# Keys and queries by a second level of seven products, and what was moved to make room for it

## The chip, the cores and the metric

The kernel runs on one core of a Trainium2 chip. The metric is the device time of one execution in microseconds (us); 2714.67 us is the median of three runs before (2713.76 to 2714.91). A core has TensorE (PE, with its weight loads shown as PEld), VectorE (DVE), ScalarE (ACT), GpSimd (POOL) and the queue of SyncE (SP), from which most DMAs are issued. The engines run side by side and wait for each other through semaphores.

## The reference

Two layers over 32 graphs (the batch b) of 512 nodes with 512 features, all in float32. The first is attention with 8 heads of 64, masked by the adjacency; the second is a graph convolution. Each is added to its input and normalized. `_layernorm(x)` takes the mean and variance of a row.

```python
def reference(x, adj, Wq, bq, Wk, bk, Wv, bv, weight, bias):
    # layer 0
    q, k, v = ((x @ W + c).reshape(b, n, 8, 64) for W, c in ((Wq, bq), (Wk, bk), (Wv, bv)))
    scores = einsum('bihd,bjhd->bhij', q, k) / sqrt(64) + where(adj == 0, -1e9, 0)
    out = einsum('bhij,bjhd->bihd', softmax(scores), v).reshape(b, n, 512)
    x = _layernorm(x + out)
    # layer 1
    norm_adj = adj * deg_inv_sqrt[:, None] * deg_inv_sqrt[None, :]
    x = _layernorm(x + einsum('nm,bmo->bno', norm_adj, x @ weight) + bias)
    return x
```

## The kernel before

Every product of two 512x512 matrices (x by Wk, Wq, Wv, and the convolution's z by W1) is done by the method of seven products: both factors are cut into four halves' blocks of 256x256, sums and differences of blocks are kept beside the blocks (slots 0 to 6 of `XT`, `wk`, `wqv`, `w1`), and seven block products take the place of eight. One of these is called a half product here. It is done by matmuls with 128 rows of weights and 256 moving columns, and its result is read out of a PSUM bank by a *put* (ACT) or an *add* (DVE) into each output block that it belongs to. The tables `CHAIN` (L325), `LEAF` (L352) and `OUTER` (L353) give the order of the products, the banks ("A", "D", "B") in which they are accumulated, and the puts and adds after each; `seven` (L360) turns a table into a list of steps.

For the values (`values_of`, L382) and for the convolution of the inner batches, four of the seven half products, those of the blocks (1,1), (3,2), (2,3) and (4,4), are each done once more by seven, on blocks of 128x128. One step does the same *quarter product* for all four, by four matmuls of 128 moving columns into one bank; seven such steps (`quarters_of`, L410, table `LEAF`) take the place of the four half products, whose factors are 128-wide quarters (`QUARTERS`, made by `quarter`, L170, and the weights' by `weigh_quarter`, L258). The other three half products follow by table `OUTER`. For keys and queries (`keys_and_queries`, L438) all seven half products are done, for r = 0 and r = 1, each with K (weights `wk`) and Q (weights `wqv`) in the two halves of one bank; ACT's put adds the bias.

Wk stays in SBUF. The buffer `wqv` holds Wq or Wv in turn; `swap(0)` and `swap(1)` (L266) load the one or the other with its sums from DRAM, on SP.

The main loop (L898) runs over b and keeps three batches in flight: attention of b, the normalization and convolution of b-1, and the second normalization and stores of b-2. One pass has four stages on TensorE:

1. the first stretch (`stretch`, L529): for two of four groups of two heads, `scores` (PE, DVE's masked copy `e`, ACT's exponential), then `values` (PE) and `unload_values` (DVE's transpose into the one buffer `yb`, and SP's DMAs from `yb` into `yT`). `accumulate` (L481) sums the numerators `e` on POOL into `acc`;
2. keys and queries of b+1. Beside them are played, at numbered steps: `rest` and `store` of b-2 (statistics, `roots`, L574, ACT's normalization, SP's stores), the addition of the residual to b-1 (`add`, POOL), the `fold` (L543, DVE) of the two sums, `measure` and `root` of b-1, `quarters` of x, `norm` (ACT, two passes), `judge` (three small instructions of DVE that check the range of `inv`) and `low` (DVE, `lo`), and the gather that adds b1;
3. the second stretch, for the other two groups;
4. the first convolution product, the values of b+1 and the second convolution product (`convolve`, L709), with the folds of the second stretch, the scaling of the attention's output by `inv` (ACT), the loads of x for b+2 and of the residual, and POOL's sums of blocks.

Within an engine the order is the order of the program text: the wrapper `InOrder` pins every instruction to it. So a waiting instruction holds all that stand behind it on its engine. Waits come from the tile framework, which follows the use of every buffer and PSUM bank. The banks are handed out in turn:

```python
    def bank(shape, name="mm"):
        psum["n"] += 1
        return psum["pool"].tile(shape, F32, name=name, tag=f"bank{-psum['n'] % 8}", bufs=1)

    def pair(name):
        return psum["pool"].tile([P, 2, N], F32, name=name, tag="pair", bufs=4)
```

`banks(kind)` closes the pool and opens the next over the same eight banks: four pairs for the scores, eight single ones for products.

Of the kernel before, what the change touches and what calls it, by code (L numbers as in the profile page):

```python
# [18 lines left out]
P = 128  # L19
# [31 lines left out]
def unshifted(  # L51
# [21 lines left out]
    LAST = B - 1  # L73
    tensor, vector, scalar, gpsimd, sync = (
# [41 lines left out]
    columns = consts.tile([P, 12, 2, DT], F32, name="columns")  # L116
    XT = consts.tile([P, 11, 2, HALF], F32, name="xT")
    QUARTERS = XT[:, 7:].rearrange("p k u o -> p k (u o)").rearrange("p k (n o) -> p k n o", o=P)
# [51 lines left out]
    def quarter(at):  # L170
        old, new = XT[:, 1:5].rearrange("p k u (t o) -> p k u t o", t=2), QUARTERS
        to, a, c = (
            (1, old[:, :, 0, 1], old[:, :, 0, 0]), (2, old[:, :, 1, 1], new[:, 1]),
            (3, old[:, :, 1, 1], old[:, :, 0, 1]), (0, old[:, :, 1, 0], new[:, 2]),
        )[at]
        gpsimd.tensor_tensor(new[:, to], a, c, ALU.subtract)

    def quarters():
        for at in range(4):
            quarter(at)  # L180

    R = {}

    def load_residual(b):
        if b < LAST:
            t = acts.tile([P, NT, D], F32, name="xr", tag="zT", bufs=1)
        else:
            t = wk[:, 3:].rearrange("p k u o -> p k (u o)")
        R[b] = [t[:, i, :] for i in range(NT)]
        for i in range(NT):  # L190
            sync.dma_start(R[b][i], x[b, ts(i, P), :])
        return [lambda: gather(t, rows(bv))]
# [11 lines left out]
    def load_parts(w, name, engine, t=None, pieces=PIECES):  # L204
        if t is None:
            t = consts.tile([P, 7, 2, HALF], F32, name=name)
        for i, q in pieces:
            engine.dma_start(
                t[32 * q : 32 * (q + 1), 2 * i : 2 * i + 2].rearrange("r j u o -> r (j u) o"),
                w[ts(q, P), ts(i, HALF)].rearrange("(t r) o -> r t o", r=32),  # L210
            )
        return t
# [11 lines left out]
    def load_row(v, name, engine):  # L224
        t = consts.tile([P, v.shape[0]], F32, name=name)
        engine.dma_start(t, bass.AP(tensor=v.tensor, offset=v.offset, ap=[[0, P], [1, v.shape[0]]]))
        return t
# [25 lines left out]
    b1_r = load_row(b1, "b1_r", nc.sync)  # L253
    wv_quarters = consts.tile([P, 3, 4, P], F32, name="wv_quarters")
    w1_quarters = consts.tile([P, 3, 4, P], F32, name="w1_quarters")
    stored = [drams.tile([P, 7, 2, HALF], F32, name=f"{name}_parts") for name in ("wq", "wv", "w1")]
# [9 lines left out]
    def swap(k):  # L266
        sync.dma_start(wqv, stored[k])
# [7 lines left out]
    minus_half = consts.tile([P, NT], F32, name="minus_half")  # L275
    gpsimd.memset(minus_half, -0.5)
    half = consts.tile([P, NT], F32, name="half")
    gpsimd.memset(half, 0.5)
    sel = consts.tile([P, 2, 32], F32, name="sel")
# [16 lines left out]
    consts.tile([P, 88], F32, name="margin")  # L296
# [85 lines left out]
    def values_of(b):  # L382
# [23 lines left out]
        left = lambda k, s: XT[:, s, k % 2, ts(k // 2, P)] if k in (0, 1, 3) else QUARTERS[:, max(k - 3, 0), s - 1]  # L406
        leaf, _ = quarters_of(left, w, wv_quarters, lambda: V[b], lambda: out(0, 0))
# [29 lines left out]

    def keys_and_queries(b, r):  # L438
        def multiply(p, i, j, fresh):
            for c, w in enumerate((wk, wqv)):  # L440
                for u in range(2):
                    tensor.matmul(
                        p[:, c, :], w[:, i, u, ts(r, P)], XT[:, j, u, :],
                        start=fresh and c == 0 and u == 0, stop=u == 1, skip_group_check=True,
                    )

        def out(i, j):
            if (b, ORDER[0]) not in KQ:
                for g in ORDER:
                    KQ[b, g] = acts.tile([P, 2, N], F32, name="kq", bufs=6)  # L450
            return KQ[b, r + 2 * i][:, :, ts(j, HALF)]

        def put(q, p):
            g = r + 2 * q[0]
            for c in range(2):
                scalar.activation(out(*q)[:, c], p[:, c], AF.Identity, bias=bias[:, c, g : g + 1], scale=1.0)

        def add(q, p):
            vector.tensor_add(out(*q), out(*q), p)

        return seven(CHAIN if b else PLAIN_FIRST, multiply, put, add)

# [17 lines left out]

    def accumulate(b, g):  # L481
        e = E[b, g]
        if b < LAST:
            a = work.tile([P, 2, N], F32, name="acc", bufs=2)
            gpsimd.tensor_add(a, e[0], e[1])
            for j in range(2, NT):
                gpsimd.tensor_add(a, a, e[j])
            ACC[b, g] = [a]
            return
        ACC[b, g] = []  # L490
        for l in range(2):
# [7 lines left out]
            ACC[b, g].append(a)  # L499

# [28 lines left out]
    def stretch(b, gs, gap=()):  # L529
# [3 lines left out]
        for g in gs:  # L533
            accumulate(b, g)
        banks("products")
        for g in gs:
            av = bank([P, N], "av")
            values(b, g, av)
            unload_values(b, g, av)
            if g == gs[0]:  # L540
                run(gap)

    def fold(b, g):  # L543
        a = ACC.pop((b, g))[0]
        if g == ORDER[0]:
            SM[b] = small.tile([P, H, N // 32], F32, name="folded")
# [26 lines left out]

    def roots(mv, eps):  # L574
# [14 lines left out]
    def finish(b):  # L589
        t = {}  # L590

        def inverse_all():
# [5 lines left out]
            t["inv"] = small.tile([P, NT, H], F32, name="inv")  # L598
# [7 lines left out]
        def inverse(c, p):  # L606
# [4 lines left out]
            if c == 0:  # L611
                t["inv"] = small.tile([P, NT, H], F32, name="inv")
# [3 lines left out]
        def judge():  # L616
            inv = t["inv"].rearrange("p i h -> p (i h)")
            low = small.tile([P, NT * H], F32, name="low")
# [38 lines left out]
        def root(i=0, k=NT):  # L657
            rstd, add = roots(t["mv"][:, i : i + k], None)
# [3 lines left out]
        def norm(i):  # L662
            if b not in HI:
                if b < LAST:
                    HI[b] = acts.tile([P, NT, D], F32R, name="hi", bufs=1)
                    lo = acts.tile([P, NT, D], F32R, name="lo", bufs=1)
                    LO[b] = [lo[:, k, :] for k in range(NT)]
                else:
                    HI[b] = acts.tile([P, NT, D], F32R, name="hi2", tag="v", bufs=1)
                    lo = [acts.tile([P, 2, D], F32R, name="lo2", tag="kq", bufs=6) for _ in range(2)]  # L670
                    LO[b] = [lo[k // 2][:, k % 2, :] for k in range(NT)]
# [37 lines left out]
    def convolve(b):  # L709
# [59 lines left out]
        def begin():  # L769
# [5 lines left out]
            if b == LAST - 2:  # L775
                t["whole"] = XT[:, 7:].rearrange("p k u o -> p k (u o)")
# [65 lines left out]
        def root(n, k):  # L842
            t[n] = roots(t["mv"][:, n : n + k], eps2[:, n : n + k])
# [43 lines left out]
    nc.sync.dma_start(stored[1], NUM[:, :4].rearrange("p e k (u o) -> p (e k) u o", u=2)[:, :7])  # L887
# [10 lines left out]
    for b in range(B):  # L898
# [7 lines left out]
        stretch(b, one, late + back["measure"][:3] if back else ())  # L906
# [12 lines left out]
        if b < LAST:  # L919
            k0, k1 = keys_and_queries(b + 1, 0), keys_and_queries(b + 1, 1)  # L920
            main = [p for pair in zip(k0, k1) for p in pair]
            if b == 0:
                ahead_x = acts.tile([P, 2, 2, N], F32, name="x2", tag="lo", bufs=1)
# [9 lines left out]
            else:  # L933
                measure, norm, low = ahead["measure"], ahead["norm"], ahead["low"]
                loads = [lambda b=b: biased.extend(load_residual(b))]
                scale = ahead["inverse"] + ahead["scale"] if b == 1 else []
                beside = {
                    0: rest + scale + ahead["add"], 1: store[:1] + fold0, 2: store[1:2], 3: store[2:3] + fold1,
                    4: store[3:] + measure[:2] + (loads if b == LAST - 1 else []), 5: measure[2:] + ahead["root"] + [quarters],
                    7: norm[:1] + ahead["judge"], 8: norm[1:2] + low[:1] + ([lambda: run(biased)] if b == LAST - 1 else []),  # L940
                    9: norm[2:3] + low[1:2], 10: norm[3:] + low[2:3],
                    11: low[3:] + ahead["lift_all"],
# [13 lines left out]
        if b < LAST:  # L956
            swap(1)
        stretch(b, two, f[b]["pairs"][0] + f[b]["pairs"][1] if b == LAST else ())
# [6 lines left out]
        if b < LAST:  # L965
            end = f[b]
            if b == 0:
                fourth = acts.tile([P, 4, P], F32, name="fourth", tag="hi", bufs=1)

                def weigh_values():  # L970
                    for k in range(4):
                        weigh_quarter(wqv, wv_quarters, k, gpsimd, fourth)
                    sync.dma_start(stored[1][:, 1:5, 0, P:], fourth)
                    weigh_quarter(w1, w1_quarters, 3, gpsimd)
# [4 lines left out]
            else:  # L979
# [13 lines left out]
                if b < LAST - 1:  # L993
                    beside = {
                        1: parts[:1] + fold0 + grow[:2], 2: grow[2:] + loads, 3: parts[1:] + conv["unjoin"] + conv["quarters"] + fold1,
                        5: end["inverse"], 7: heads[:14], 11: heads[14:23], 13: conv["open"], 16: turn0,
# [4 lines left out]
                else:  # L1001
                    measure, norm, low = end["measure"], end["norm"], end["low"]
                    biased = load_residual(LAST)
# [3 lines left out]
                        15: measure[:1], 16: measure[1:2], 17: measure[2:3], 18: measure[3:] + end["root"],  # L1007
# [7 lines left out]
    count = small.tile([P, 1], F32, name="count")  # L1015
    ones = small.tile([P, 1], F32, name="ones")
# [18 lines left out]
    bad = small.tile([1, 1], I32, name="bad")  # L1035
# [288 lines left out]
```

## Time and profile before

| what | value |
|---|---|
| median of three runs | 2714.67 us |
| the profiled execution: time / span | 2714.88 / 2712.5 us |
| granted clock | 0.998 |
| PE busy | 2688.3 us, 99% (13956 matmul records) |
| PEld busy | 1917.1 us, 71% |
| DVE busy | 1986.2 us, 73% |
| ACT busy | 1522.3 us, 56% |
| POOL busy | 2078.5 us, 77% |
| DMA | 324.05 MB, mean 119 GB/s |

The span reaches from the first to the last instruction; the execution's own time is 2.38 us longer. Busy times are unions over an engine's instructions. A matmul of the program is two records in the trace, and these overlap, so the time from start to start counts and not the duration that a row gives. In the answers below a row of the timeline has the start, the length, the engine, the line (always L45, the wrapper), the operation, the written and read tiles, the shapes and the count; in brackets is the idle time before it and what ended it. A tile's row has the least, median and greatest duration in ns.

### The profile page before, as it was taken

The numbers are of one execution on the slowest core, as the hardware profiler recorded it, in microseconds if no ns is written. First come the engines' busy times: TensorE is split into PE (matmuls) and PEld (weight loads), VectorE is DVE, ScalarE is ACT, GpSimd is POOL, SyncE is SP. The second block draws the span as 40 slices with busy tenths as digits, with TensorE's granted clock in tenths as the row PEclk, the third lists the DMA queues.
The fourth block names the chain that finished last, engine by engine and source line by source line (L and its number), as shares of the span: only waits on it lengthen the run. The fifth ranks groups of instructions, "written<-read, shape, count | busy, mean of one in ns | idle before, by whom it ended". The sixth has DMA issues, their size and how long they took to land. (4 is left out here: it accounts for less than half of the span.)

```text
span 2712.5 us, 39096 instructions
## 1 busy us (share of the span) xinstructions
PE 2688.3 (99%) x13956; PEld 1917.1 (71%) x13956; DVE 1986.2 (73%) x2743; ACT 1522.3 (56%) x2825; POOL 2078.5 (77%) x1380
## 2 busy tenths in 40 slices
PE   9999999999999999999999999999999999999997
PEld 6677676776776766767767677677676676776765
DVE  4777777777777777767777777777777776777777
ACT  3456555565555565555655556555556555565564
POOL 4778778777787777877877877778777787787765
PEclk9999999999999999999999999999999999999999
DMA  6344445545445454455444544544545445544541
GB/s 187 121 110 121 113 105 136 132 106 124 113 126 127 111 134 115 105 130 122 125 113 105 136 132 105 121 121 120 127 111 135 114 105 131 124 123 113 130 100 48
DMA packets 421994, 324.05 MB, mean 119 GB/s; under 512 B 279840, under 2 KB 348448, under 8 KB 413600
## 3 DMA queue, kind: packets, MB, share of 16 engines
q1 hardware_dynamic: 388048, 255.14, 30.3%
q0 software_dynamic: 32736, 65.02, 15.5%
q8 instruction: 113, 1.85, 0.3%
q10 hardware_dynamic: 1008, 1.31, 0.2%
q14 instruction: 89, 0.73, 0.1%
HBM read 248.78 MB, written 39.32 MB: 106 GB/s over the span
## 5 line engine op out<-in xcount | busy, mean ns | idle before, releaser
L45 DVE SCALAR_TENSOR_TENSOR e<-sc,maskT 128x1024 f32<-128x1024 f32 x512 | 585.1, 1216 | 101.2 <-PE sc L45 101.2
L45 ACT ACTIVATE e<-e 128x1024 f32<-128x1024 f32 x512 | 540.9, 1058 | 115.3 <-DVE e L45 84.6
L45 POOL TENSOR_TENSOR acc<-acc,e 128x1024 f32<-128x1024 f32 x248 | 589.5, 2377 | 19.4
L45 PE MATMUL mm<-xT,wk 128*128 128x256 f32 x1792 | 463.1, 381 | 0.0
L45 PE MATMUL mm<-xT,wqv 128*128 128x256 f32 x1792 | 459.9, 379 | 0.0
L45 POOL TENSOR_TENSOR acc<-e 128x1024 f32<-128x1024 f32 x126 | 297.2, 2359 | 209.3 <-ACT e L45 209.3
L45 PE MATMUL sc<-kq 64*128 64x512 f32 x2048 | 457.2, 596 | 0.0
L45 PE MATMUL av<-e,v 128*64 128x512 f32 x2048 | 453.6, 595 | 0.3
L45 POOL TENSOR_TENSOR xT<-xT 128x512 f32<-128x512 f32 x246 | 353.1, 1445 | 90.0 <-DVE xT L45 58.0
L45 PEld LDWEIGHTS mm<-xT,wk 128*128 128x128 f32 x1792 | 337.6, 190 | 69.8 <-DVE mv L45 23.5
L45 ACT ACTIVATE kq<-mm,bias 128x256 f32<-128x256 f32 x512 | 214.0, 472 | 288.7 <-PE mm L45 288.5
L45 PEld LDWEIGHTS mm<-xT,wqv 128*128 128x128 f32 x1792 | 340.5, 190 | 46.3
L45 POOL TENSOR_TENSOR e<-e 128x512 f32<-128x512 f32 x240 | 303.6, 1276 | 73.5 <-ACT e L45 57.9
L45 PEld LDWEIGHTS av<-e,v 128*64 128x64 f32 x2048 | 148.7, 137 | 297.9 <-issue 231.2
L45 PEld LDWEIGHTS sc<-kq 64*128 64x128 f32 x2048 | 192.1, 186 | 233.2 <-issue 176.8
L45 PE MATMUL mm<-wqv,xT 128*128 128x256 f32 (+1 forms) x1736 | 304.3, 321 | 0.0
L45 PE MATMUL mm<-w,e 128*128 128x128 f32 (+1 forms) x1680 | 297.9, 323 | 0.0
L45 DVE STREAM_TRANSPOSE yb<-av 128x512 f32<-128x512 f32 x127 | 91.0, 717 | 258.4 <-DMA yT<-yb 167.0
L45 PEld LDWEIGHTS mm<-wqv,xT 128*128 128x128 f32 x1736 | 264.1, 191 | 21.6 <-issue 0.8
L45 PEld LDWEIGHTS mm<-w,e 128*128 128x128 f32 x1680 | 253.4, 191 | 25.0 <-DVE y L45 7.1
L45 DVE TENSOR_TENSOR v<-v,mm 128x512 f32<-128x512 f32 x217 | 146.5, 687 | 151.8 <-ACT v L45 76.5
L45 ACT ACTIVATE yT<-yT,inv 128x64 f32<-128x64 f32 x960 | 238.9, 338 | 0.0
(143 smaller groups left out, 3462.3 us busy)
## 6 DMA issues: line engine op xcount, KB each, us to landing
wqv<-wv_parts SPq DMA_DIRECT2D x31, 1792.0 KB, 11.7
wqv<-wq_parts SPq DMA_DIRECT2D x30, 1792.0 KB, 10.0
yT<-yb SPq DMA_DIRECT2D x508, 64.0 KB, 2.4
xr<-in_L_gnn_bv_dram POOLq DMA_DIRECT2D x31, 1024.0 KB, 11.0
xr<-in_x_dram SPq DMA_DIRECT2D x122, 256.0 KB, 4.3
e<-in_x_dram SPq DMA_DIRECT2D x240, 128.0 KB, 2.8
yT<-in_L_gnn_bias_dram POOLq DMA_DIRECT2D x30, 1024.0 KB, 14.2
out_dram<-y SPq DMA_DIRECT2D x120, 256.0 KB, 2.0
```

The costliest lines, as they stand in the source:

```text
L45: return self.tc.keep_in_program_order(op(*args, **kwargs))
```

## The change

Keys and queries of the batches 2 to 31 (made in the passes b = 1 to 30) are done as the values are: seven quarter products and three half products for K, and as many for Q, by the new `keys_or_queries`. The biases are added by DVE with the half products' results. `wk` and `wqv` get ten slots, of which three hold the weights' quarters, and the swaps carry ten slots. Of the fourth quarter, both x and the weights now write it in place. The four groups' K and Q lie in one tile, `KQ_RING`.

Several pieces change their stage. x's `quarters` and the residual's addition go ahead of the first stretch; three of the first stretch's six sums stay there, and the others go between the products of stage 2; the folds of the first two groups go from stage 2 into the second stretch, between its two transposes; `judge` goes from stage 2 into stage 4; the residual's loads go from step 2 to step 5 of stage 4. The second stretch's sums lie in buffers of their own (`acc2`, in the space of `xr`). `roots_beside` does on POOL what `roots` does on DVE and POOL. In pass 0 the weights' quarters are made and stored.

```diff
-    XT = consts.tile([P, 11, 2, HALF], F32, name="xT")
-    QUARTERS = XT[:, 7:].rearrange("p k u o -> p k (u o)").rearrange("p k (n o) -> p k n o", o=P)
+    XT = consts.tile([P, 10, 2, HALF], F32, name="xT")
+    QUARTERS = quarters_in(XT)
...
+    wk_quarters, wqv_quarters = quarters_in(wk), quarters_in(wqv)
...
-    def swap(k):
-        sync.dma_start(wqv, stored[k])
+    def swap(k, slots=10):
+        sync.dma_start(wqv[:, :slots], stored[k][:, :slots])
...
+    KQ_RING = acts.tile([P, 6, 2, N], F32, name="kq", bufs=1)
...
+    def keys_or_queries(b, c):
+        w, w_quarters = ((wk, wk_quarters), (wqv, wqv_quarters))[c]
+
+        def multiply(p, i, j, fresh):
+            for r in range(2):
+                for u in range(2):
+                    tensor.matmul(
+                        p[:, r, :], w[:, i, u, ts(r, P)], XT[:, j, u, :],
+                        start=fresh and r == 0 and u == 0, stop=u == 1, skip_group_check=True,
+                    )
+
+        def multiply_quarters(p, i, j, fresh):
+            for n, (k, l) in enumerate(((1, 1), (3, 2), (2, 3), (4, 4))):
+                part = w[:, k, i % 2, ts(i // 2, P)] if i < 4 else w_quarters[:, i - 4, k - 1]
+                tensor.matmul(p[:, n, :], part, left_x(j, l), start=fresh and n == 0, stop=True, skip_group_check=True)
...
+        def put(q, p):
+            scalar.copy(quarter_of(*q), p.rearrange("p (j i) o -> p j i o", i=2))
+
+        def add(q, p):
+            vector.tensor_add(quarter_of(*q), quarter_of(*q), p.rearrange("p (j i) o -> p j i o", i=2))
+
+        def spread_last():
+            for r in range(2):
+                gpsimd.tensor_add(rows(r, 0, 1), rows(r, 0, 1), rows(r, 1, 1))
+
+        def add_outer(q, p):
+            for r in range(2):
+                to, g = rows(r, *q), r + 2 * q[0]
+                vector.scalar_tensor_tensor(to, p[:, r, :], bias[:, c, g : g + 1], to, op0=ALU.add, op1=ALU.add)
+
+        leaf = seven(LEAF, multiply_quarters, put, add, (4, P))
+        return leaf, [spread_last], seven(OUTER, multiply, None, add_outer)
...
-    def stretch(b, gs, gap=()):
+    def stretch(b, gs, gap=(), sums=6):
...
-        for g in gs:
-            accumulate(b, g)
+        pieces = accumulations(b, gs)
+        run(pieces[:sums])
...
+        return pieces[sums:]
...
+    def roots_beside(mv, eps):
+        k = mv.shape[1]
+        ve = small.tile([P, k], F32, name="ve")
+        gpsimd.tensor_tensor(ve, mv[:, :, 1], eps1[:, :k] if eps is None else eps, ALU.add)
+        low = small.tile([P, k], F32, name="nmu")
+        gpsimd.tensor_tensor(low, mv[:, :, 0], minus_one[:, :k], ALU.mult)
+        rstd = small.tile([P, k], F32, name="rstd")
+        gpsimd.tensor_tensor(rstd, ve, minus_half[:, :k], ALU.pow)
+        add = small.tile([P, k], F32, name="add")
+        gpsimd.tensor_tensor(add, low, rstd, ALU.mult)
+        return rstd, add
...
-        stretch(b, one, late + back["measure"][:3] if back else ())
+        if 0 < b < LAST:
+            quarters()
+            if b > 1:
+                run(ahead["add"])
+        gap = ahead["inverse"] + ahead["scale"] if b == 1 else late + back["measure"][:3] if back else ()
+        more = stretch(b, one, gap, 3 if b else 6)
+        if b == 1:
+            run(ahead["add"])
...
+                (k_leaf, k_spread, k_outer), (q_leaf, q_spread, q_outer) = (keys_or_queries(b + 1, i) for i in range(2))
+                main = (
+                    k_leaf[:6] + k_outer[:1] + k_leaf[6:] + k_outer[1:2] + q_leaf[:6] + q_outer[:1] + q_leaf[6:]
+                    + q_outer[1:2] + k_outer[2:3] + q_outer[2:3] + k_outer[3:] + q_outer[3:]
+                )
...
                 beside = {
-                    0: rest + scale + ahead["add"], 1: store[:1] + fold0, 2: store[1:2], 3: store[2:3] + fold1,
-                    4: store[3:] + measure[:2] + (loads if b == LAST - 1 else []), 5: measure[2:] + ahead["root"] + [quarters],
-                    7: norm[:1] + ahead["judge"], 8: norm[1:2] + low[:1] + ([lambda: run(biased)] if b == LAST - 1 else []),
-                    9: norm[2:3] + low[1:2], 10: norm[3:] + low[2:3],
-                    11: low[3:] + ahead["lift_all"],
+                    0: loads if b == LAST - 1 else [], 2: rest[:1], 5: rest[1:] + more[:1] + measure[:2],
+                    6: store[:2] + measure[2:3], 7: store[2:3],
+                    8: measure[3:] + more[1:2] + ahead["root"] + ([lambda: run(biased)] if b == LAST - 1 else []),
+                    9: store[3:], 10: k_spread + more[2:], 12: norm[:1], 13: norm[1:2], 14: low[:1], 15: low[1:2],
+                    16: norm[2:3], 17: norm[3:] + q_spread, 18: low[2:3], 19: low[3:] + ahead["lift_all"],
                 }
...
-        if b < LAST:
+        if b == 0:
+            weigh_quarter(wqv, wqv_quarters, 3, gpsimd)
+            sync.dma_start(stored[0][:, 1:5, 0, P:], wqv[:, 1:5, 0, P:])
+            swap(1, 7)
+        elif b < LAST:
             swap(1)
-        stretch(b, two, f[b]["pairs"][0] + f[b]["pairs"][1] if b == LAST else ())
+        stretch(b, two, f[b]["pairs"][0] + f[b]["pairs"][1] if b == LAST else fold0 + fold1 if b else ())
...
-                        1: parts[:1] + fold0 + grow[:2], 2: grow[2:] + loads, 3: parts[1:] + conv["unjoin"] + conv["quarters"] + fold1,
-                        5: end["inverse"], 7: heads[:14], 11: heads[14:23], 13: conv["open"], 16: turn0,
+                        1: parts[:1] + fold0 + grow[:2], 2: grow[2:], 3: parts[1:] + conv["unjoin"] + conv["quarters"] + fold1,
+                        5: end["inverse"] + loads, 7: heads[:14], 11: heads[14:23], 13: conv["open"] + ahead["judge"], 16: turn0,
```

## The prediction, made before the change was run

> **What bounds the kernel now.** I read the page first: TensorE is busy 2688.3 of 2712.5 us, every slice is at 9 tenths, and the granted clock is 0.998. So the time is TensorE's own work plus whatever it waits. The kernel is periodic; the table of stretches cuts one period of 83.47 us into its four stages (columns: length, then busy time and count of PE, PEld, DVE, ACT, POOL, then clock, DMA share, GB/s).
>
> ```profile
> 1033.92:1048.01 14.09, 14.09 (x66) 5.29 (x65) 12.82 (x16) 9.04 (x9) 11.55 (x6) 1.00 0.55 164
> 1048.01:1072.38 24.37, 24.37 (x115) 21.20 (x113) 20.00 (x32) 14.16 (x26) 19.51 (x16) 1.00 0.22 60
> 1072.38:1086.47 14.09, 14.09 (x66) 5.31 (x65) 9.86 (x9) 9.30 (x10) 9.22 (x4) 1.00 0.86 215
> 1086.47:1117.39 30.92, 30.92 (x197) 27.85 (x196) 19.08 (x27) 15.38 (x45) 25.30 (x20) 1.00 0.46 104
> ```
>
> The second row is the stage of keys and queries: PE has no gap, but DVE, ACT and POOL are 82%, 58% and 80% busy beside it. Then the timeline of PE, for the price of a half product, of a quarter product and of the step into the scores:
>
> ```profile
> 1013.30 1.06 PE L45 MATMUL mm<-wv_quarters,xT 128*128 128x128 f32 x8
> 1014.20 1.06 PE L45 MATMUL mm<-wqv,xT 128*128 128x128 f32 x8
> ...
> 1070.56 1.03 PE L45 MATMUL mm<-xT,wk 128*128 128x256 f32 x4
> 1071.42 1.03 PE L45 MATMUL mm<-xT,wqv 128*128 128x256 f32 x4
> 1072.38 7.14 PE L45 MATMUL sc<-kq 64*128 64x512 f32 x32
> ```
>
> Starts count, not durations, since matmuls overlap: eight 128-wide ones take 0.90 us (0.893 over longer rows), four 256-wide 0.86, so 0.1116 and 0.2157 us each. The scores follow the last product at once.
>
> POOL and ACT set when the next steps can start:
>
> ```profile
> 1035.41 1.27 POOL L45 TENSOR_TENSOR y<-y,side 128x512 f32<-128x512 f32 x1 [0.45 <-ACT side L45]
> 1038.62 2.38 POOL L45 TENSOR_TENSOR acc<-e 128x1024 f32<-128x1024 f32 x1 [1.94 <-ACT e L45]
> 1041.07 4.83 POOL L45 TENSOR_TENSOR acc<-acc,e 128x1024 f32<-128x1024 f32 x2
> ...
> 1054.28 0.20 POOL L45 TENSOR_TENSOR add<-nmu,rstd 128x4 f32<-128x4 f32 x1
> 1054.43 4.96 POOL L45 TENSOR_TENSOR yT<-yT,xr 128x512 f32<-128x512 f32 x4
> ```
>
> ```profile
> 1062.79 0.81 ACT L45 ACTIVATE yT<-yT,add,rstd 128x512 f32<-128x512 f32 x1 [2.46 <-POOL add L45]
> 1063.64 0.72 ACT L45 ACTIVATE hi<-yT,dis 128x512 fp32r<-128x512 f32 x1
> ```
>
> ACT's norm starts as soon as POOL's `add` of the roots is out, and a row of it (yT, hi) takes 1.5 us. In before this happens 14.8 us into the stage. A last view, of tiles and forms:
>
> ```profile
> L45 DVE TENSOR_SCALAR low<-inv x32: 174/1222/1244, 147.7 to 2691.4; 128x32 f32<-128x32 f32 x32
> L45 DVE SCALAR_TENSOR_TENSOR yT<-mm,inv,wk x8: 273/276/278, 2665.6 to 2671.2; 128x64 f32<-128x64 f32 x8
> ```
>
> [...]`low<-inv` over 32 elements has minimum 174 and median 1222 ns, about one POOL instruction more.
>
> **The change part by part.** Let T be the start of the keys-and-queries stage, S = T - 14.1 that of the scores before it.
>
> PE. Per batch 64 of 112 instructions of 256 columns become 112 of 128: 112 x 0.1116 + 48 x 0.2157 = 22.85 us, against 24.37. This is done for the 30 batches 2 to 31: 30 x 1.52 = 45.6 us less work for PE.
>
> The last adds. In before, the seven products were put by ACT (16 of 0.47 us) and DVE (6 adds of 0.68). Now DVE has 6 adds of 0.68 and 16 scalar_tensor_tensor of 128x256 out of PSUM, which before does not show. [...] Back to back, rows overlap by some 0.08[...]; I take 0.40. The order of the built instructions puts the four adds of K's last product and the four of Q's at the end, and the first score matmul of the second stretch waits for the last of these eight: its bank is the one that holds Q's outer products. In before nothing there waited for DVE. If no one else is late, PE ends at T+22.85, Q's four adds run from 0.2 later (as ACT's put after a product does in before), and the scores start at 22.85 + 0.2 + 1.6 + 0.08 = T+24.7: 0.36 **later** than before, whatever PE saved.
>
> The late roots. POOL's new order after the side add (S+1.5): side 1.27; x's quarters 4 x 1.27 = 5.1 (moved here); the residual adds 5.0 (moved here); first sums 7.24; roots of b-2, now four POOL instructions, 0.35 + 1.1 + 0.2 = 1.65; two of the deferred sums 4.85; roots of b-1 1.65. Sum 26.8, so X = S+28.3 = T+14.2, without a gap to absorb anything. ACT then needs 3.05 for two norms; DVE's queue holds lo, lo (each 1.0) ahead of the two outer adds of Q, so these end at X+5.0 = T+19.2. Q's second outer product writes the bank that they read and would start at T+17.7 (18.3 with what the first roots delay ACT's puts of Q). PE stalls until T+19.2; three products later it ends at T+24.4; DVE has lo (to T+23.0), K's four adds to 24.6, Q's to 26.2: scores at T+26.3. Against 24.37 that is +1.93 a batch, 30 x 1.93 = **+57.9 us**. [...]
>
> The judgement of `inv` (three DVE instructions, 1.65 us at the median, 0.55 at least) moves from the middle of the keys-and-queries stage to just ahead of the first adds of y in the values stage. There an add started at 1020.14 for a matmul at 1021.39: 0.49 us of room. So 0.06 to 1.16 us for 29 batches; I take 0.6: **+17 us**.
>
> Edits at nothing, with their cover: the folds of the first two groups move into the second stretch, where DVE has 14.09 - 9.86 us idle and its second transpose waited for the yb transfer anyway (until S+16.2 there, 16.3 now); ve and nmu leave DVE (1.47 us median) for POOL and are counted in X; the spreads (four 128x256 on POOL, between the 128x4 row 0.2 and the 128x512 row 1.27, 0.66 each) end at X+5.1, before DVE needs them. DMAs: the swaps grow from 1792 to 2560 KB, on SP, 61 times; by size 10.0 becomes 14.3 and 11.7 becomes 16.7 us; they are due 22 and 21.3 us after issue. The yb transfers behind them on SP may land some us later; DVE's adds have 0.8 us there. The residual loads move three steps down SP and wait for the folds; their gather (11.0 us to landing, issued at S-6.3) lands 3 us before POOL adds it.
>
> Start, once: the fourth quarter of Wq, its 256 KB store (2.2 us by `fourth`) and then the swap lie between two stages; in before the swap landed at 100.5, due at 102.8. Plus 1.4 + 2.2: **+2 us** (0 to 4). The six extra POOL quarters lie in its 27.6 us of idleness.
>
> Sum, on the profiled execution's 2714.88 us (span 2712.5 and 2.4 around it; the median of the runs is 2714.67): +57.9 + 17 + 2 = **2792 us**.
>
> **Rivals.**
> Only the last adds hold: if POOL's chain reached X by T+12.6, PE would not stall inside the stage, and 30 x 0.36 + 2 gives 2728. Against it: the chain has 26.8 us of rows in 28.3.
> Faster: the scores' wait and the stall stay under 1.52 us a batch together, because DVE drains its adds in the shadow of PE; at zero, 2714.9 - 45.6 + 2 = 2671. It decides at 4 adds plus latency = 1.52, i.e. 0.31 us an add; for it speaks that DVE's mean share has 27% free[...].
> Worse: the judgement waits a whole POOL instruction each time (+34 instead of 17), or the larger swaps push yb and with it DVE: 2810 to 2832.
> The change doing nothing is excluded: 720 more matmuls stand in the built order, each of them two records of the trace.
>
> **Chances.** The forecast with its worse form 0.70, the last adds alone 0.15, faster 0.10, a balance within 0.2% (5.4 us, about what a measurement of this kernel tells from no change) 0.05. Slower 0.85. The range runs from 2720, below the last adds alone, to 2832.
>
> **What would show it.** Right: [...]PEld sc waiting for DVE kq about 1.9 us a period; PEld mm waiting for DVE kq one to two us; the roots' second `add` near T+14; POOL over 83% busy; PE busy share down. Wrong: scores following PE's last product at once, or Q's second outer product at T+17.7; a period under 83.47 us.

## The result, and the profile after

The changed kernel takes **2815.58 us** (median of 4 runs, 2814.97 to 2817.78) against 2714.3 us (2713.76 to 2714.91): a ratio of 1.0375, 95% interval 1.0357 to 1.0393. It is slower by 101 us; the forecast was 2792 with a range of 2720 to 2832. The span of the profiled execution is 2813.2 us, 100.7 more than before.

The first part of the page of the changed kernel, engine by engine (busy time, share of the span, instructions):

```profile
PE 2680.4 (95%) x15396; PEld 1942.6 (69%) x15396; DVE 2157.4 (77%) x3105; ACT 1462.3 (52%) x2585; POOL 2186.0 (78%) x1628
```

PE's busy share fell from 99% to 95%: the new time is waiting on PE, not work. The table of stretches says in which stage (columns as before: length, busy time and count of PE, PEld, DVE, ACT, POOL, clock, DMA share, GB/s):

```profile
1071.50:1085.59 14.09, 14.09 (x66) 5.25 (x65) 12.82 (x16) 9.04 (x9) 13.48 (x11) 1.00 0.67 219
1085.59:1112.94 27.35, 23.81 (x162) 21.67 (x161) 20.38 (x37) 13.00 (x20) 20.74 (x19) 1.00 0.23 59
1112.94:1127.03 14.09, 14.09 (x65) 5.60 (x65) 12.39 (x12) 8.46 (x8) 9.23 (x4) 1.00 0.89 261
1127.03:1158.07 31.04, 31.04 (x196) 27.89 (x194) 21.48 (x32) 15.39 (x45) 25.39 (x20) 1.00 0.46 104
```

The period is 86.57 us instead of 83.47. Of the 3.10 us, 2.98 are in the second row, keys and queries, where PE is idle for 27.35 - 23.81 = 3.54 us; 0.12 are in the fourth. PE's timeline of that stage, and its end:

```profile
1085.59 8.36 PE L45 MATMUL mm<-xT,wk 128*128 128x128 f32 x64
1093.78 8.47 PE L45 MATMUL mm<-xT,wqv 128*128 128x128 f32 x64
1102.08 1.89 PE L45 MATMUL mm<-xT,wk 128*128 128x256 f32 x8
1105.65 1.99 PE L45 MATMUL mm<-xT,wqv 128*128 128x256 f32 x8 [1.68 <-DVE kq L45]
...
1109.21 1.89 PE L45 MATMUL mm<-xT,wqv 128*128 128x256 f32 x8
1112.94 1.56 PE L45 MATMUL sc<-kq 64*128 64x512 f32 x6 [1.84 <-DVE kq L45]
```

With T = 1085.59, Q's second outer product starts at T+20.06 after a wait, and the scores start at T+27.35 after another. Both wait for `kq` of DVE, in nearly all of the 30 passes, as the list of waits has it (total us, times, longest):

```profile
PE mm L45 <- DVE kq L45: 55.2, 30, 4.3
...
PE sc L45 <- DVE kq L45: 53.5, 29, 1.8
```

DVE and POOL in the same microseconds:

```profile
1101.08 3.73 DVE L45 SCALAR_TENSOR_TENSOR lo<-yT,dis,hi 128x512 fp32r<-128x512 f32 x2 [0.73 <-ACT hi L45]
1104.73 1.65 DVE L45 SCALAR_TENSOR_TENSOR kq<-mm,bias,kq 128x256 f32<-128x256 f32 x4
...
1109.41 3.39 DVE L45 SCALAR_TENSOR_TENSOR kq<-mm,bias,kq 128x256 f32<-128x256 f32 x8
```

```profile
1099.24 0.20 POOL L45 TENSOR_TENSOR add<-nmu,rstd 128x4 f32<-128x4 f32 x1
...
1100.77 2.36 POOL L45 TENSOR_TENSOR acc<-acc,e 128x1024 f32<-128x1024 f32 x1
```

Two `lo` take 3.73 us where I had counted 2.0, and Q's adds stand behind them in DVE's queue. A narrow window shows the first alone:

```profile
1101.08 2.60 DVE L45 SCALAR_TENSOR_TENSOR lo<-yT,dis,hi 128x512 fp32r<-128x512 f32 x1 [0.73 <-ACT hi L45]
```

It starts 0.3 us after POOL's deferred sum (`acc`) and ends at 1103.68, 0.55 us after that sum. The eight instructions in the row at 1109.41 are the adds of the last products, and the scores follow them. That DVE is late in both places is read; why is a matter for experiments.

### The profile page after: what moved, and what is told of

Same layout as the page of the kernel before. It is cut to its first block, busy times and chain, and to the rows that moved or that the text cites. A ratio compares the mean times of both kernels' runs of the same rounds, so it can differ in the third digit from the quotient of the medians.

```text
span 2813.2 us, 42389 instructions
## 1 busy us (share of the span) xinstructions
PE 2680.4 (95%) x15396; PEld 1942.6 (69%) x15396; DVE 2157.4 (77%) x3105; ACT 1462.3 (52%) x2585; POOL 2186.0 (78%) x1628
## 3 DMA queue, kind: packets, MB, share of 16 engines
q10 hardware_dynamic: 1008, 1.31, 0.1%
## 4 chain that ended last, share of the span: by engine, by line
PE 61%; POOL 26%; DVE 6%; issue 4%; ACT 2%; DMA 0%; POOLq 0%; SPq 0%; DVEq 0%; ACTq 0%
PE mm L45 43%; POOL acc L45 12%; PE sc L45 9%; PE av L45 9%; POOL yT L45 5%; POOL xT L45 4%; DVE kq L45 3%; DVE lo L45 2%; POOL rstd L45 2%; POOL y L45 1%; ACT yT L45 1%; ACT hi L45 1%; DVE y L45 1%; ACT side L45 1%; POOL add L45 0%
## 5 line engine op out<-in xcount | busy, mean ns | idle before, releaser
L45 PE MATMUL mm<-xT,wqv 128*128 128x256 f32 (+1 forms) x2512 | 401.7, 314 | 55.9 <-DVE kq L45 55.2
L45 PEld LDWEIGHTS mm<-xT,wqv 128*128 128x128 f32 x2512 | 351.1, 192 | 94.2 <-DVE kq L45 67.2
L45 PE MATMUL mm<-xT,wk 128*128 128x256 f32 (+1 forms) x2512 | 393.9, 312 | 1.4 <-POOL yT L45 1.4
L45 PEld LDWEIGHTS sc<-kq 64*128 64x128 f32 x2048 | 203.8, 186 | 277.0 <-issue 222.0
L45 POOL TENSOR_TENSOR xT<-xT 128x512 f32<-128x512 f32 x246 | 326.8, 1334 | 76.9 <-DVE xT L45 42.5
L45 PEld LDWEIGHTS mm<-xT,wk 128*128 128x128 f32 x2512 | 348.2, 191 | 48.1 <-DVE mv L45 23.5
L45 PE MATMUL mm<-wqv,xT 128*128 128x128 f32 (+1 forms) x2456 | 376.4, 308 | 0.2 <-DVE v L45 0.2
L45 PEld LDWEIGHTS mm<-wqv,xT 128*128 128x128 f32 x2456 | 341.0, 191 | 22.2 <-issue 0.8
L45 DVE SCALAR_TENSOR_TENSOR kq<-mm,bias,kq 128x256 f32<-128x256 f32 x480 | 203.3, 475 | 41.7 <-PE mm L45 25.4
L45 ACT COPY kq<-mm 128x512 f32<-128x512 f32 x240 | 138.2, 576 | 171.4 <-PE mm L45 169.6
## 6 DMA issues: line engine op xcount, KB each, us to landing
wqv<-wq_parts SPq DMA_DIRECT2D x30, 2560.0 KB, 11.9
wqv<-wv_parts SPq DMA_DIRECT2D x30, 2560.0 KB, 13.6
```

Of the source, the lines that this page charges most:

```text
L45: return self.tc.keep_in_program_order(op(*args, **kwargs))
```

## The experiments

**Theories.** Mine: two waits of PE, independent of each other. (a) Q's second outer product waits for DVE's adds, which stand behind two `lo`; these are late because the roots come late on POOL, and because POOL's third deferred sum holds `lo` up. (b) The first scores wait for the last add because of the bank that they are handed. Rivals: the time of the roots alone sets (a); the wait of (b), taken away, comes back in the scores, since DVE's adds must be done anyway; the quarter products or the larger swaps cost PE more than the matmul starts show.

**1. The third sum away from `lo`.** In the table `beside` of stage 2:

```diff
-                    9: store[3:], 10: k_spread + more[2:], 12: norm[:1], ...
-                    ... 19: low[3:] + ahead["lift_all"],
+                    9: store[3:], 10: k_spread, 12: norm[:1], ...
+                    ... 19: low[3:] + ahead["lift_all"] + more[2:],
```

> Only the third deferred sum (acc<-acc,e, 128x1024, 2.36 us on POOL) is moved, from ahead of Q's spread to behind the gather at the end of the stage; the roots' add stays at T+13.85. Theory (the sum holds DVE's two lo up): the two lo take 1.5 us together instead of 3.73, Q's second outer product no longer waits (1.68 to about 0), the keys-and-queries stage falls from 27.35 to 25.4-25.7 us, the kernel to about 2765 us (2755 to 2775); the wait of the first scores (1.84) stays. Rival (the roots' chain alone sets Q's adds, the lo are slow for another reason): lo, stall and stage as they are, 2815 us.

Measured: 2770.05 us (ratio to the kernel before 1.0215, 1.0198 to 1.0232). DVE's and POOL's timelines:

```profile
1083.67 0.96 DVE L45 SCALAR_TENSOR_TENSOR lo<-yT,dis,hi 128x512 fp32r<-128x512 f32 x1 [0.73 <-ACT hi L45]
1085.13 0.75 DVE L45 SCALAR_TENSOR_TENSOR lo<-yT,dis,hi 128x512 fp32r<-128x512 f32 x1 [0.50 <-ACT hi L45]
```

```profile
1081.83 0.20 POOL L45 TENSOR_TENSOR add<-nmu,rstd 128x4 f32<-128x4 f32 x1
```

The sum that stood beside `lo` is no longer there. The stage starts at 1068.12 here, so the roots' `add` starts at T+13.71, as in the changed kernel (T+13.65). The two `lo` are 0.96 and 0.75 us, and the stage is 25.89 us. With unchanged roots 1.5 us a batch are gone: the sum beside `lo` cost them. The stage is 0.2 us above what I expected, the time within it. The wait of Q's second outer product is not quite nothing, 0.16 us in PE's timeline.

**2. The roots first.** Both later sums go behind the gather:

```diff
-                    8: measure[3:] + more[1:2] + ahead["root"] + ...
+                    8: measure[3:] + ahead["root"] + ...
...
+                    ... 19: low[3:] + ahead["lift_all"] + more[1:],
```

> The second and third deferred sums both go behind the gather at the end of the stage, so that nothing stands between the roots of b-2 and those of b-1 on POOL. Theory (late roots and the sum beside lo both count): the roots' add comes at T+12.3, lo and lo are done by T+16, Q's adds by T+17.7; no stall or 0.3 at most, stage 24.7-25.2 us with the wait of the first scores still in it, 2735 to 2750 us. Rival (only the time of the roots counts, 1.55 us earlier): stage 25.8, about 2772 us. Rival (quarter products cost PE more than their starts show): stage stays above 27, over 2805 us.

Measured: 2750.30 us (1.0136, 1.0119 to 1.0153), 20 us less than experiment 1. The table of stretches and the wait ahead of the scores, in PE's timeline:

```profile
1060.68:1086.12 25.44, 23.57 (x162) 21.78 (x161) 18.25 (x37) 13.11 (x20) 17.21 (x18) 1.00 0.24 63
```

```profile
1086.12 7.14 PE L45 MATMUL sc<-kq 64*128 64x512 f32 x32 [1.84 <-DVE kq L45]
```

No wait is left inside the stage; the one ahead of the scores is as it was, 1.84 us. So the two waits are separate. The time is just above the upper edge of what I expected (2750), the stage 0.24 us above its own (25.2): the quarter products take more than I had counted, see below.

**3. Other banks.** The banks of the outer products are opened before the leaf products, so that they are the fourth pair of the scores instead of part of the first:

```diff
+        held = {"A": bank([P, 2, HALF])}
         leaf = seven(LEAF, multiply_quarters, put, add, (4, P))
-        return leaf, [spread_last], seven(OUTER, multiply, None, add_outer)
+        return leaf, [spread_last], seven(OUTER, multiply, None, add_outer, regions=held)
```

> The banks of K's and Q's outer products are opened ahead of the leaf products, nothing else is changed: they then fall to the fourth pair of the scores and the first three pairs are free when PE comes. Theory: the wait of the first scores (1.84) goes, the stall of Q's second outer product (1.68) stays; stage 25.5 us, the scores behind it unchanged at 14.1, 2763 us (2758 to 2775). Rival (DVE's first e stands behind Q's last adds anyway, so the wait moves to the fourth or fifth pair): stage 25.5, but the scores' stretch grows to 15.3 or more, 2800 us or more.

Measured: 2777.52 us (1.0238, 1.0221 to 1.0255), 2.5 us above the range. The table of stretches, stage 2 and the scores behind it:

```profile
1072.38:1097.87 25.49, 23.77 (x162) 21.68 (x161) 18.70 (x33) 13.00 (x20) 20.76 (x19) 1.00 0.21 59
1097.87:1112.46 14.59, 14.49 (x66) 5.49 (x65) 14.04 (x17) 8.46 (x8) 9.26 (x5) 1.00 0.91 260
```

The stage is as expected; the stretch is 0.50 us longer. DVE's timeline has why:

```profile
1096.25 3.39 DVE L45 SCALAR_TENSOR_TENSOR kq<-mm,bias,kq 128x256 f32<-128x256 f32 x8
1099.55 9.13 DVE L45 SCALAR_TENSOR_TENSOR e<-sc,maskT 128x1024 f32<-128x1024 f32 x8
```

The scores start at 1097.87, but the first `e` stands behind the adds until 1099.55. Neither text was right alone: the bank caused 1.84 us of waiting, and a quarter of it comes back, since the program writes a bank of the scores again only when DVE has read it. That this is what stretches them is argued here; experiment 6 has a test of it.

**4. Both together**, and in pass 30 the residual's gather moved from step 8 to step 19.

> The second and the third experiment together, and in batch 30 the gather of the residual behind the last lo too. Theory (the two waits are separate and PE's saving is real): stage 22.9-23.3 us against 24.37 in the kernel before, 2685 to 2700 us, faster than before. Rival (PE's saving is eaten by something other than the two waits, the swaps or the weight loads of 128 columns): stage not under 24.4, 2725 us or more.

Measured: 2714.46 us (1.0003, 0.9994 to 1.0012), no difference from the kernel before. The waits are gone and the stage is 23.53 us, under 24.37, so PE's saving is real, but the rest of the expected gain is missing. Three things took it. The stage is 23.53 us and not 22.9 to 23.3. The scores are longer by 0.5 us, as in experiment 3. And pass 30 lost some 5 us: by the starts of PE's groups its last stage takes 36.90 us, against 31.71 in experiment 6, where the gather is back at step 8. POOL's sums behind the gather came later, then DVE's folds, and PE waited for them (PE's timeline of pass 30):

```profile
2597.48 0.77 PE L45 MATMUL mm<-folded,spread 128*128 128x128 f32 x2 [3.34 <-DVE folded L45]
```

**5. Fewer adds behind the last product.** In the changed kernel, the two adds of the last outer product in each half, which have the same input and bias, become one:

```diff
+            if q == (1, 0):
+                return
...
+                if q == (1, 1):
+                    to = KQ[b, g][:, c].rearrange("p (j o) -> p j o", j=2)
+                    part = p[:, r, None, :].to_broadcast([P, 2, HALF])
+                vector.scalar_tensor_tensor(to, part, bias[:, c, g : g + 1], to, op0=ALU.add, op1=ALU.add)
```

> The changed kernel with one edit: the last product's two adds per half (two scalar_tensor_tensor of 128x256 with the same PSUM input and bias) become one of 128x512 that reads the PSUM half twice. Theory (the first scores wait for the last of DVE's adds, which run back to back): one of 512 takes 0.69 us where two of 256 take 0.84, so the four adds behind Q's last product become two, 1.38 instead of 1.68; the wait of the first scores falls from 1.84 to 1.55 us, the stage from 27.36 to 27.05, the kernel by 9 us to about 2806. Rival (the scores wait for something else, the bank of a leaf or ACT): wait and stage unchanged, 2815 us.

Measured: 2810.71 us (ratio 1.0358, 1.0342 to 1.0374). The intervals of this ratio and of the changed kernel's overlap, so the time alone decides nothing (it is 4.9 us less, where I expected 9); the timelines of DVE and PE do:

```profile
1111.03 1.41 DVE L45 SCALAR_TENSOR_TENSOR kq<-mm,bias,kq 128x512 f32<-128x512 f32 x2 [0.32 <-PE mm L45]
```

```profile
1112.59 3.70 PE L45 MATMUL sc<-kq 64*128 64x512 f32 x16 [1.59 <-DVE kq L45]
```

Two adds take 1.41 us, and the wait of the scores falls from 1.84 to 1.59: it is DVE's last add that they wait for.

**6. All that the experiments point to.** Experiments 2, 3 and 5, with `judge` in a gap of DVE and the gather of pass 30 back at step 8:

```diff
-                        ... 11: heads[14:23], 13: conv["open"] + ahead["judge"], ...
+                        ... 11: ahead["judge"] + heads[14:23], 13: conv["open"], ...
```

> The second, third and fifth experiment together, with the judgement of inv moved from step 13 to step 11 of the values stage, where DVE waits 2.5 us for ACT's v. In batch 30 the gather of the residual stands where the changed kernel has it. Against the fourth experiment: the values stage 0.12 us shorter (30.93-30.95), the second scores 14.3 instead of 14.59, the end of batch 30 3 to 4 us shorter; keys and queries 23.5. About 2697 us (2692 to 2704), faster than before by over 0.4%. If DVE's tail is not what stretches the scores they stay at 14.59 and the time is about 2706.

Measured: 2696.43 us (0.9934, 0.9921 to 0.9948). By the starts of PE's groups, keys and queries take 23.49 us, the second scores 14.33 and the values stage 30.84: each within 0.1 us of what was expected. That the scores fall from 14.59 to 14.33, with half as many instructions in DVE's tail, shows that this tail is what stretched them.

**7. One row of the store two steps later.**

```diff
-                    9: store[3:], 10: k_spread, 12: norm[:1], ...
+                    10: k_spread, 11: store[3:], 12: norm[:1], ...
```

> As the sixth, with the last row of the store of y (ACT 0.72 us and its DMA) two steps later, at step 11. PE has a wait of 0.29 us in Q's fourth leaf product, which I put down to ACT's copy of Q's second product standing behind the rows of y. Theory: that wait goes, keys and queries 23.25, about 2690 us. Rival: ACT's norm of b-1 comes later by the same 0.7 us and Q's outer products wait for it: stage 23.5 or more, 2697 us or more.

Measured: **2689.09 us** (0.9906, 0.9891 to 0.9922), 25 us faster than the kernel before. PE's timeline:

```profile
1123.62 8.36 PE L45 MATMUL mm<-xT,wk 128*128 128x128 f32 x64
1131.82 8.22 PE L45 MATMUL mm<-xT,wqv 128*128 128x128 f32 x64
1139.88 1.89 PE L45 MATMUL mm<-xT,wk 128*128 128x256 f32 x8
...
1146.88 3.70 PE L45 MATMUL sc<-kq 64*128 64x512 f32 x16
```

From Q's first start to K's next group are 8.06 us here and 8.30 in the changed kernel and in experiment 6; the stage is 23.26 us, 0.23 less than in experiment 6. So 0.24 us of waiting in Q's leaf products was ACT's copy standing behind the rows of y.

## Why the prediction was right, and where it was off

The direction and the mechanism held: two waits of PE for DVE, inside the stage and at its end, cost more than PE saved. The time lay in the range, 24 us above the forecast. That it came so near is in part luck, as the sum below shows. Point by point:

- **The last adds: right.** I took 0.40 us an add, an estimate of mine that no row of before showed; eight take 3.39 us, 0.42 each. The scores were to start 1.9 us after PE's last product. By the starts that product ends at 1109.21 + 8 x 0.2157 = 1110.94, and the scores start 2.00 us later. Experiments 3 and 5 show bank and adds as the cause. In the changed kernel one add lasts 0.48 us (median 476 ns), and where adds stand back to back they start 0.39 us apart (median of 301 pairs).
- **The time of the roots: right.** X was to be T+14.2 and is T+13.85 (the end of `add` at 1099.44). One sign that went with it did not show: POOL was to be over 83% busy and is 78%, against 77% before. In experiment 2 X comes at T+12.6 with POOL at 79%, so it was the order of the work on POOL that set X, and not the share.
- **"lo, lo (each 1.0)": the mis-sized term.** They took 3.73 us, so Q's adds ended near T+20 and not T+19.2. In the prediction I counted what POOL does beside it for `judge` alone. The traces show it for `lo` too: 2.60 us beside the deferred sum, 0.75 with POOL idle, as in experiment 2. They also show for how long. In the changed kernel 62 of the 128 `lo` begin while an addition of POOL runs, with 0.33 to 2.29 us of it left, and 61 of them end 0.54 to 0.55 us after that addition. (The other is in pass 30, see below.) The kernel before, where the 1.0 came from, shows the same:

```profile
1064.06 1.32 POOL L45 TENSOR_TENSOR xT<-xT 128x512 f32<-128x512 f32 x1
1064.98 0.96 DVE L45 SCALAR_TENSOR_TENSOR lo<-yT,dis,hi 128x512 fp32r<-128x512 f32 x1
```

  POOL's row ends at 1065.38 and `lo` at 1065.94, 0.56 us later. So the mean of 1.0 told how much of a POOL instruction was left where `lo` stood, and beside a longer sum it had to be more. The adds out of PSUM were not held: 118 of the 480 in the changed kernel begin while an addition of POOL runs, with 0.20 to 2.15 us of it left, and their median is 470 ns against 476 of the others. The tile's row there (least, median, greatest ns of the 480):

```profile
L45 DVE SCALAR_TENSOR_TENSOR kq<-mm,bias,kq x480: 451/476/486, 140.6 to 2675.8; 128x256 f32<-128x256 f32 x160
```

- **PE's nominal 22.85: too low, but not what made the stage longer than forecast.** The two leaf groups each hold 56 starts of 128 columns and 8 of 256, 56 x 0.1116 + 8 x 0.2157 = 7.98 us; they take 8.19 and 8.30, together 0.53 us more. I had priced the matmuls and no short wait between products. In the changed kernel the stall hides this, since Q's second outer product starts when DVE's adds are done. The stage ends at T+27.35 and not T+26.3: 0.86 us because that product starts at T+20.06 and not T+19.2, and 0.19 because the eight adds take 3.39 us and not 3.2. The short waits count once the stall is gone, as in experiment 2. Experiment 7 shows that 0.24 us of them was ACT's copy in Q's leaf. Another 0.10 is the step into the stage, which the kernel before has too (its first four starts take 0.97 us, the next four 0.86); what the rest waits for was not taken apart.
- **PE's saving of 1.52 a batch: too high from the start.** 22.85 is a sum of starts, while the 24.37 beside it was measured. By the same prices the stage of before is 112 x 0.2157 = 24.16 us, so the saving was 1.31, and 39 us in 30 batches instead of 45.6. With no wait left for DVE the stage is 23.53 us in experiment 4 and 23.26 in experiment 7: 0.84 to 1.11 a batch came out.
- **`judge`: too dear, and for a reason that was not foreseen.** The values stage grew by 0.12 us and not 0.6. The first of the three instructions has a median of 182 ns now against 1222. POOL does not rest there; the instruction begins close to the end of one of POOL's sums of blocks:

```profile
1142.96 1.28 POOL L45 TENSOR_TENSOR e<-e 128x512 f32<-128x512 f32 x1
1144.09 0.18 DVE L45 TENSOR_SCALAR low<-inv 128x32 f32<-128x32 f32 x1
```

  The sum has 0.15 us left, and `low` ends some 0.04 us after it. In experiment 6 `low` begins early in one of the same sums, and there it is held, again until some 0.04 us after the end:

```profile
1096.61 1.27 POOL L45 TENSOR_TENSOR e<-e 128x512 f32<-128x512 f32 x1
1097.09 0.84 DVE L45 TENSOR_SCALAR low<-inv 128x32 f32<-128x32 f32 x1
```

  In before it begins 0.09 us after the start of one of the sums for x's quarters, and it is held for nearly the whole of it, 1.22 us. So in all three places `low` ends some 0.04 us after POOL's instruction, and its length is what was left of that instruction and these 0.04 us. The step that failed is that I carried a duration from one neighbour to another.
- **The start: wrong.** I took +2 us; the values of batch 1, which the swap feeds, start at 102.52 us against 102.77 before. I had put that swap's landing in before at 100.5. The trace has it 7.4 us after its issue at 88.78, so at 96.2; in the changed kernel it is issued at 91.71 and lands 7.0 us later, still 3.8 us early.
- **The swaps: landed sooner** than by size, 11.9 and 13.6 us in the median instead of 14.3 and 16.7, and no wait for them appeared.
- **Two passes were left out of the sum.** In pass 1 four `yT<-yT,inv` on DVE took 8.21 us beside POOL's sums; in pass 30 the two `lo` took 6.37 beside spreads, a sum and a gather, the first of them 5.71. By the starts of PE's groups these passes cost 6.6 and 8.15 us more than before, up to their values stages. This is read from the trace; no experiment tested it.

The sum measured: 28 passes x 2.98 = 83.4, pass 1 6.6, pass 30 8.15, the values stage 29 x 0.12 = 3.5, the start -0.2, everything behind pass 30's second stretch -1.0: 100.4 us of the 100.7 in the span, against 77 predicted. The misses went both ways. The stage was taken 28 x 1.05 = 29 us too short and the two passes together 11 us; `judge` was taken 13.5 us too dear, the start 2 and the end 1. That they left only 24 us is luck.

Of the rivals in the prediction, "only the last adds" is what experiment 2 comes near to (2750 us; the 22 us above that rival's 2728 are mostly the waits between leaf products). "Faster" was open, but not for the reason given: it took other banks and another order on POOL.

## What to carry to other kernels

When work moves from the busiest engine to its neighbours, list for each wait of the busiest engine the last instruction ahead of the release, and price that instruction with what runs beside it on the other engine, not by its median elsewhere. Where it is held by the other engine, as `lo` (2.60 us against 0.75) and `low` (1.22 against 0.18) were here, ask how much of that engine's instruction will be left when it begins. A buffer rotation can put the one bank that is read last under the first thing that is needed next; opening it earlier took that wait of 1.84 us away here. And after a wait is taken away, look at the stretch behind it: part of the time may come back there, as a quarter of this one did.

## What the runs showed of the hardware that was not expected

- A VectorE `lo` of 128x512 that began while a GpSimd addition ran ended 0.54 to 0.56 us after that addition, whether 0.33 or 2.29 us of it were left (61 of 62 in the changed kernel, 91 of 92 in before, where the one left began 0.02 us ahead of the next addition and ended 0.55 us after that one; where none ran it took 0.73 to 0.75 us). So its end moved with the end of the addition, as if it was held for the rest of it and not slowed throughout. `low<-inv` of 128x32 ended about 0.04 us after a GpSimd addition of 128x512 that it began beside (31 of 31 and 30 of 30). The deferred sum beside `lo` was not longer than the others (2.36 us, median of all 2.37).
- Eight VectorE instructions of 128x256 with one input in PSUM took 3.38 us (experiment 4) while GpSimd's sums had begun beside them; in the changed kernel, without a sum, it is 3.39.
- A PSUM half read twice by a broadcast in one instruction of 512: two such take 1.41 us (experiment 5), where four instructions of 256 take 1.65 (changed kernel).
